# A step's maxima ahead of the last step's scaling in VectorE's order (context attention of a two-layer decoder)

## The chip, the cores and the metric

The kernel runs on one core of one Trainium2 chip. A core has five engines that run beside each other, each in its own order: TensorE (PE, with its weight loads PEld), VectorE (DVE), ScalarE (ACT), GpSimd (POOL) and SyncE (SP), which issues transfers. They wait for each other by semaphores. The metric is the device time of one execution in microseconds (us); the median of three runs is compared.

## What is computed

The reference is a decoder of two layers, each made of self-attention, attention with a context and a feed-forward part, every one followed by a layer norm. The input x is 8 sequences of 512 tokens and 256 features in float32, the context 8 sequences of 64 tokens. The second layer's feed-forward part is a mixture of 8 experts of which each token takes 2. The part that matters here is the second layer's context attention: the keys and values of a sequence are joined with those of its context, so a token attends to 512 + 64 positions, with 8 heads of 64.

```python
def _L1_xattn_ref(x1, x2, Wq1, Wk1, Wv1, Wk2, Wv2, Wo, bo):
    ...
    q1 = split_heads(x1 @ Wq1, N1)
    k1 = split_heads(x1 @ Wk1, N1)
    v1 = split_heads(x1 @ Wv1, N1)
    k2 = split_heads(x2 @ Wk2, N2)
    v2 = split_heads(x2 @ Wv2, N2)
    k = jnp.concatenate([k1, k2], axis=1)
    v = jnp.concatenate([v1, v2], axis=1)
    sim = jnp.einsum('bihd,bjhd->bhij', q1.astype(jnp.float32), k.astype(jnp.float32)) * scale
    attn = jax.nn.softmax(sim, axis=-1)
    out = jnp.einsum('bhij,bjhd->bihd', attn, v)
    out = out.reshape(B, N1, h * d)
    return out @ Wo + bo
```

Around it stands `x = _layernorm(x + _L1_xattn_ref(...))`, and then the experts' part, which begins with a norm of its own and a router: two experts of each token by the greatest of 8 probabilities.

## The kernel before, in words

The stage is the phase "l1_context". It works in 128 steps n = 16b + 4c + i: sequence b (0 to 7), pair of heads c (0 to 3), tile i of 128 tokens (0 to 3). In this text (b,c,i) is such a step. The phase is scheduled by hand: on TensorE, VectorE, ScalarE and GpSimd the instructions run in the order in which the program writes them. A step is written so:

- l1x_scaling of step n-1: VectorE takes the reciprocals of the two heads' sums (L1261) and multiplies their probabilities by them, 128 x 576 each, in place (L1263, in the helper `scaled`).
- l1x_scores of step n: TensorE computes the scores of two heads (L1560), each 128 x 576 in two halves, into two PSUM tiles "s"; VectorE takes the negated maximum of each head (nm, L1564).
- l1x_transposes of step n-2, with the exponentials of step n in between: TensorE transposes the 128 context columns (L1586), and ScalarE copies them out (L1587). Then ScalarE makes the exponentials of both heads out of PSUM, with their sums (l1x_exps, L1570). Then TensorE transposes the 512 other columns of each head (L1592); VectorE copies out the first head's, ScalarE the second's (L1593).
- for i below 3, l1x_project: one of queries, keys and values of the next pair of heads (L1525, L1539; copied by ScalarE; for the keys VectorE adds the context's, L1534). For i = 3, l1x_values: the product with the values (L1602, L1607) of the pair of heads before this one, ready two steps earlier.
- side work of single steps. In (b,2,2) l1_turn transposes the next sequence's x, in two groups of four (L1065, copied by ScalarE). The list `aside` brings, for the sequence that has just ended, l1x_out and the router: in the next sequence at (0,3) a sum on GpSimd; at (1,0) and (1,1) the output product o_out (L1646) with the sum and the statistics on VectorE (L1648, L1619, L1620, L1623); from (1,2) to (2,1) two norms on VectorE (L1632 and its like); at (2,2) route_transposes (tZ, L1709, two groups, copied by ScalarE); at (2,3) route_odds (o_r, L1724); at (3,0) to (3,2) shares, picks and seconds on VectorE; at (3,3) route_places: TensorE's o_rank (L1779, L1782), VectorE's ranks down to row numbers (L1784 to L1792) and, on GpSimd's queue, eight scatters of token rows to rows_in (L1794). The sequence before the last follows a denser list, in which tZ comes at step 120, o_r at 121, o_rank at 124, and the first table of the experts' tiles in the steps behind it.

What sets the order around the change are PSUM's banks. The ring "s" has two tiles, and a step's scores take both, so the scores of step n+1 wait until both exponentials of step n have read theirs. The ring "t" has three tiles, and a step's transposes take all three: the context columns first, then the two heads; side work takes the next ones in turn. So whatever takes a fourth and fifth tile in a step needs those of the context columns and of the first head, which VectorE's copy frees. The tile of probabilities p has four buffers, the columns nm, sums and rsum four each.

After the phase the experts' phase loads rows of rows_in (L1926) and weights for 71 tiles, each with an up product (L1958) and a down product (L1975). Its first loads wait for the scatters.

Of the kernel before, what the change touches and what calls it, by code (L numbers as in the profile page):

```python
# [50 lines left out]
def decoder_kernel(ctx: ExitStack, tc: tile.TileContext, a: dict, out: bass.AP):  # L51
# [31 lines left out]
    def phase(name):  # L83

        return tc.tile_pool(name=name, bufs=2, side="right", reuse_waits="tile")
# [4 lines left out]
    def s_tile(name):  # L90
        return pp["s"].tile([P, 2, 512], F32, tag="s", name=name)
# [206 lines left out]
    def p_tile(n=S, bufs=3):  # L298
        return ph.tile([P, 2, n], F32, tag="p", name="p", bufs=bufs)
# [4 lines left out]
    def col(name, n):  # L304
        return work.tile([P, n], F32, tag=name, name=name, bufs=4)
# [801 lines left out]
    with phase("l0_context_ffn") as ph, tc.manual_schedule(engines=ALL):  # L1107
# [8 lines left out]
        steps_ = [(b, i) for b in range(NB) for i in range(NT)]  # L1116
# [33 lines left out]
        for n in range(2 * NT, len(steps_) + 3):  # L1150
            b, i = n // NT, n % NT
# [353 lines left out]
    def l1x_context_values(b):  # L1505

        o = t_tile("o_v2").rearrange("p i n -> p (i n)")
        for kc in range(KC):
            pe.matmul(o, lhsT=ctxT[:, kc, b * S2 : (b + 2) * S2], rhs=wv2[:, kc, :], start=(kc == 0), stop=(kc == KC - 1))
        both = work.tile([P, S], F32, tag="lat", name="both")  # L1510
        act.copy(both, o)
        for n in range(2):
            vx = vxs[(b + n) % 4]
            for j in range(2):
                heads = [t.rearrange("p (h two n) -> p h two n", two=2, n=S2)[:, :, j, :] for t in (vx, both)]
                sp.dma_start(out=heads[0][S2 * j : S2 * (j + 1)], in_=heads[1][S2 * n : S2 * (n + 1)])

    def l1x_project(b, c, what):

        xT = live["xT", b]  # L1520
        cols = slice(c * P, (c + 1) * P)
        o = o_tile("o_qkv")
        if what < 2:
            for kc in range(KC):
                pe.matmul(o, lhsT=(wq1, wk1)[what][:, kc, cols], rhs=xT[:, kc, :], start=(kc == 0), stop=(kc == KC - 1))  # L1525
        if what == 0:
            q = ph.tile([P, S], F32, tag="q", name="q")
            act.mul(q, o, 0.125)
            live["q", b, c] = q
        elif what == 1:  # L1530
            k = ph.tile([P, S + 2 * S2], F32, tag="k", name="k")
            act.copy(k[:, S2 : S2 + S], o)
            for h, at in ((0, S2 + S), (64, 0)):
                dve.tensor_copy(k[h : h + 64, at : at + S2], k2[h : h + 64, c, b * S2 : (b + 1) * S2])  # L1534
            live["k", b, c] = k
        else:
            for j in range(NT):
                for kc in range(KC):
                    pe.matmul(  # L1539
                        o[:, j * P : (j + 1) * P],  # L1540
                        lhsT=xT[:, kc, j * P : (j + 1) * P],
                        rhs=wv1[:, kc, cols],
                        start=(kc == 0),
                        stop=(kc == KC - 1),
                    )
            v = ph.tile([P, NT, P], F32, tag="vc", name="vc", bufs=3)
            act.copy(v.rearrange("p j n -> p (j n)"), o)
            live["v", b, c] = v

    def l1x_scores(b, c, i):  # L1550
        q, k = live["q", b, c], live["k", b, c]
        p = p_tile(S + S2, bufs=4)
        sums = col("sums", 4)
        nm = col("nm", 2)
        ss = [s_tile("s_sc")[:, :, 0:HALF] for _ in range(2)]
        for t in range(2):
            for j, s in enumerate(ss):
                h = 64 * j
                at = S2 * (1 - j) + HALF * t
                pe.matmul(  # L1560
                    s[:, t, :], lhsT=q[h : h + 64, i * P : (i + 1) * P], rhs=k[h : h + 64, at : at + HALF], start=True, stop=True
                )
        for j, s in enumerate(ss):
            dve.tensor_reduce(nm[:, j : j + 1], s, AX.XY, ALU.max, negate=True)  # L1564
        live["s", b, c, i] = ss, p, sums, nm
# [9 lines left out]
    def l1x_scaling(b, c, i):  # L1575
        p, sums = live["p", b, c, i]
        scaled(p, sums, S + S2)

    def l1x_transposes(b, c, i, meanwhile):
        p, _ = live.pop(("p", b, c, i))  # L1580
        p = p.rearrange("p j n -> p (j n)")
        if i == 0:
            live["pt", b, c] = pts[c % 2], ph.tile([P, S], F32, tag="pt2", name="pt2")
        pt, pt2 = live["pt", b, c]
        t = t_tile("tP2")[:, 0, :]
        pe.transpose(t, p[:, S : S + P], ident)  # L1586
        act.copy(pt2[:, i * P : (i + 1) * P], t)  # L1587
        meanwhile()
        for j, copy in ((0, dve.tensor_copy), (1, act.copy)):
            t = t_tile("tP")  # L1590
            for k in range(NT):
                pe.transpose(t[:, k, :], p[:, (S + P) * j + k * P : (S + P) * j + (k + 1) * P], ident)  # L1592
            copy(pt[j][:, :, i * P : (i + 1) * P], t)  # L1593
# [413 lines left out]
    with phase("l1_context") as ph, tc.manual_schedule(engines=ALL):  # L2007
        vxs = [ph.tile([P, S], F32, name=f"vx{n}", bufs=1) for n in range(4)]
        for vx in vxs:
            pool.memset(vx, 0.0)  # L2010
        steps_ = [(b, c, i) for b in range(NB) for c in range(4) for i in range(NT)]
        aside = {}
        l1x_context_values(0)
        for what in range(3):
            l1x_project(0, 0, what)
        for n in range(len(steps_) + NT):
            b, c, i = n // (4 * NT), n // NT % 4, n % NT
            if 1 <= n <= len(steps_):
                l1x_scaling(*steps_[n - 1])
            if n < len(steps_):  # L2020
                l1x_scores(b, c, i)
            meanwhile = partial(l1x_exps, b, c, i) if n < len(steps_) else nothing
            if 2 <= n < len(steps_) + 2:
                l1x_transposes(*steps_[n - 2], meanwhile)
            else:
                meanwhile()
            if i < 3:
                nb, nc_ = (b, c + 1) if c < 3 else (b + 1, 0)
                if nb < NB:
                    l1x_project(nb, nc_, i)  # L2030
            elif n >= NT:
                pb, pc = steps_[n - NT][:2]
                l1x_values(pb, pc)
                if pc == 3 and pb < NB - 1:
                    after = [
                        *l1x_out(pb),
                        *(partial(f, pb) for f in (route_transposes, route_odds, route_shares, route_picks, route_seconds, route_places)),
                    ]
                    ats = list(range(len(after)))
                    if pb == NB - 2:  # L2040
                        ats = [0, 1, 2, 3, 3, 4, 4, 5, 6, 7, 7, 8, 9, 10, 11, 12, 13, 13]
                        early_pieces = early_blocks()
                        after.extend([lambda: next(early_pieces, None)] * 4)
                        after.extend(partial(moe_load, m, tables_rows) for m in range(AHEAD))
                    for at, piece in zip(ats, after):
                        aside.setdefault(n + at, []).append(piece)
            if (c, i) == (2, 2) and b + 1 < NB:
                for kc in range(KC):
                    l1_turn(b + 1, kc)
            if (b, c, i) == (NB - 1, 2, 1):  # L2050
                last = l1x_out(b)
                last.pop(0)()
            if (c, i) == (1, 1) and b % 2 and b + 1 < NB:
                l1x_context_values(b + 1)
            for piece in aside.pop(n, []):
                piece()
        for n in sorted(aside):
            for piece in aside[n]:
                piece()
        for piece in last[:4]:  # L2060
            piece()
        last_route.extend(
            [
                lambda: (last[4](), last[5]()),
                nothing,
                nothing,
                partial(route_transposes, NB - 1),
                lambda: (route_odds(NB - 1), route_shares(NB - 1)),
                lambda: (route_picks(NB - 1), route_seconds(NB - 1)),
                partial(route_places, NB - 1),  # L2070
            ]
        )
# [139 lines left out]
```

## Time and profile before

| what | us |
|---|---|
| median of three runs | 3152.14 (3150.56 to 3152.29) |
| the profiled execution | 3156.77 |
| its span, first to last instruction | 3155.1 |
| TensorE busy | 3063.9 (97%) |
| VectorE busy | 1920.7 (61%) |
| ScalarE busy | 1642.3 (52%) |
| GpSimd busy | 1101.3 (35%) |

The groups of the page that belong to the steps of this stage, with the line, the engine, what is written from what, the count, then busy us and mean ns of one, then idle us of the engine ahead of them and what ended it:

```profile
L1263 DVE TENSOR_SCALAR p<-p,rsum 128x576 f32<-128x576 f32 (+4 forms) x768 | 297.1, 429 | 13.6
L1570 ACT ACTIVATE p<-s_sc,nm 128x576 f32<-128x576 f32 x256 | 187.4, 737 | 101.8 <-DVE nm L1564 101.1
L1564 DVE TENSOR_REDUCE nm<-s_sc 128x1 f32<-128x576 f32 x256 | 181.4, 750 | 73.2 <-PE s_sc L1560 73.2
L1560 PE MATMUL s_sc<-k,q 64*128 64x288 f32 x1024 | 174.2, 433 | 9.7 <-ACT p L1570 9.7
```

L1263 is a helper's line that the self-attention uses too: 256 of the 768 are this stage's. An idle time is charged to the engine that waited, not to the end of the program; whether it counts is seen in the chain of waits, which follows the last instruction back to what released each one.

### The profile page before, as it was taken

The numbers are of one execution on the slowest core, as the hardware profiler recorded it, in microseconds if no ns is written. First come the engines' busy times: TensorE is split into PE (matmuls) and PEld (weight loads), VectorE is DVE, ScalarE is ACT, GpSimd is POOL, SyncE is SP. The second block draws the span as 40 slices with busy tenths as digits, with TensorE's granted clock in tenths as the row PEclk, the third lists the DMA queues.
The fourth block names the chain that finished last, engine by engine and source line by source line (L and its number), as shares of the span: only waits on it lengthen the run. The fifth ranks groups of instructions, "written<-read, shape, count | busy, mean of one in ns | idle before, by whom it ended". The sixth has DMA issues, their size and how long they took to land.

```text
span 3155.1 us, 54217 instructions
## 1 busy us (share of the span) xinstructions
PE 3063.9 (97%) x19598; PEld 2029.3 (64%) x19598; DVE 1920.7 (61%) x6331; ACT 1642.3 (52%) x3507; POOL 1101.3 (35%) x992
## 2 busy tenths in 40 slices
PE   8999999999999999999999999999999999999995
PEld 3444444455666677677767765666666558888885
DVE  6888888876553767767677746766766773110112
ACT  4555555557664666766676656555545543222222
POOL 5988888934432222222222210011111112221222
PEclk8999999999999999999999999999999999999998
DMA  5000111101006963333332310000000016766674
GB/s 165 28 28 28 41 45 44 35 6 43 6 3 170 255 132 48 41 41 41 42 45 38 42 43 1 16 16 25 22 18 21 21 51 210 226 193 180 185 238 148
DMA packets 170975, 235.25 MB, mean 75 GB/s; under 512 B 31915, under 2 KB 134059, under 8 KB 170709
## 3 DMA queue, kind: packets, MB, share of 16 engines
q1 hardware_dynamic: 144692, 179.91, 18.2%
q0 software_dynamic: 25584, 51.57, 11.5%
q8 instruction: 155, 2.54, 0.3%
q14 instruction: 112, 0.91, 0.1%
q10 hardware_dynamic: 432, 0.33, 0.0%
HBM read 136.03 MB, written 61.12 MB: 62 GB/s over the span
## 4 chain that ended last, share of the span: by engine, by line
PE 83%; DVE 6%; ACT 4%; DMA 2%; SPq 2%; issue 1%; POOL 0%; POOLq 0%; DVEq 0%; ACTq 0%
PE o_y L1975 7%; PE s_h L1958 7%; PE s_sc L480 5%; PE s_sc L1560 4%; PE o_pv L1345 4%; PE s_sc L1283 4%; PE tP L1332 4%; PE o_pv L576 4%; PE o_out L1369 4%; PE o_out L1039 3%; PE o_pv L1602 3%; PE s_q L1080 3%; PE o_qkv L1525 3%; PE tP L1592 3%; PE s_h L1015 2%; PE s_st L556 2%
## 5 line engine op out<-in xcount | busy, mean ns | idle before, releaser
L565 ACT ACTIVATE pt<-s_st 128x1024 f32<-128x1024 f32 x256 | 248.3, 1022 | 263.5 <-PE s_st L561 263.5
L1101 POOL DMA_DIRECT2D qk<-turned x256 | 202.8, 1168 | 520.2 <-PE tP L1332 319.4
L489 DVE CUSTOM_DVE_ANT_0 scored<-s_sc,decay 128x512 f32<-128x512 f32 x492 | 314.5, 686 | 54.3 <-PE s_sc L480 52.5
L1310 ACT ACTIVATE p<-p,nm 128x128 f32<-128x128 f32 (+3 forms) x512 | 282.6, 554 | 61.4 <-DVE nm L1296 61.4
L1263 DVE TENSOR_SCALAR p<-p,rsum 128x576 f32<-128x576 f32 (+4 forms) x768 | 297.1, 429 | 13.6
L1296 DVE CUSTOM_DVE_ANT_0 p<-s_sc,tabs 128x128 f32<-128x128 f32 (+3 forms) x512 | 215.6, 487 | 124.9 <-PE s_sc L1283 124.9
L1995 DVE TENSOR_SCALAR y<-o_y,share 128x256 f32<-128x256 f32 x71 | 34.2, 483 | 403.3 <-PE o_y L1975 403.3
L1958 PE MATMUL s_h<-xnT,we 128*128 128x256 f32 (+1 forms) x1248 | 258.8, 361 | 0.0
L1975 PE MATMUL o_y<-we,h 128*128 128x256 f32 x1136 | 251.4, 379 | 0.0
L1996 POOL DMA_INDIRECT total<-y,to x71 | 109.8, 1546 | 386.2 <-DVE y L1995 193.4
L1570 ACT ACTIVATE p<-s_sc,nm 128x576 f32<-128x576 f32 x256 | 187.4, 737 | 101.8 <-DVE nm L1564 101.1
L1975 PEld LDWEIGHTS o_y<-we,h 128*128 128x128 f32 x1136 | 215.3, 190 | 29.0
L1958 PEld LDWEIGHTS s_h<-xnT,we 128*128 128x128 f32 x1248 | 215.4, 190 | 23.9 <-ACT xnT L1937 0.2
L1564 DVE TENSOR_REDUCE nm<-s_sc 128x1 f32<-128x576 f32 x256 | 181.4, 750 | 73.2 <-PE s_sc L1560 73.2
L1332 PEld LDWEIGHTS tP<-ident,p 128*128 128x128 f32 x1280 | 144.8, 141 | 82.6 <-PE s_sc L1283 41.7
L480 PE MATMUL s_sc<-k,q 32*128 32x512 f32 x1024 | 188.9, 648 | 6.0 <-DVE mx L489 4.9
L1794 POOL DMA_INDIRECT rows_in<-z,irow x64 | 63.2, 988 | 374.2 <-DVE hit L1789 267.1
L1560 PE MATMUL s_sc<-k,q 64*128 64x288 f32 x1024 | 174.2, 433 | 9.7 <-ACT p L1570 9.7
L1332 PE MATMUL tP<-ident,p 128*128 128x128 f32 x1280 | 175.2, 276 | 0.1
L1937 ACT ACTIVATE xnT<-tZ,gb 128x256 f32<-128x256 f32 (+1 forms) x78 | 42.6, 546 | 237.5 <-PE tZ L1936 237.5
L1283 PE MATMUL s_sc<-qk 64*128 64x128 f32 (+3 forms) x1024 | 157.5, 443 | 3.8 <-DMA qk<-turned 3.3
L1965 ACT ACTIVATE h<-s_h 128x1024 f32<-128x1024 f32 x71 | 72.7, 1024 | 155.7 <-PE s_h L1958 155.7
(341 smaller groups left out, 6456.0 us busy)
## 6 DMA issues: line engine op xcount, KB each, us to landing
we<-in_mo_w SPq DMA_DIRECT2D x78, 1024.0 KB
rows_in<-zero SPq DMA_DIRECT2D x64, 530.0 KB
qk<-turned POOLq DMA_DIRECT2D x256, 128.0 KB, 4.3
coef<-in_ff_upw SPq DMA_DIRECT2D x40, 256.0 KB
coef<-in_ff_dnw SPq DMA_DIRECT2D x40, 256.0 KB
xr<-rows_in SPq DMA_DIRECT2D x32, 265.0 KB
x<-in_x SPq DMA_DIRECT2D x8, 512.0 KB
total<-x SPq DMA_DIRECT2D x8, 512.0 KB
```

Of the source, the lines that this page charges most:

```text
L480: pe.matmul(pairs[h // 2][:, h % 2, :], lhsT=q[r, i * P : (i + 1) * P], rhs=k[r, :], start=True, stop=True)
L489: dve.tensor_tensor_reduce(out=rows_[h], in0=pairs[h // 2][:, h % 2, :], in1=decay[:, i, :], scale=1.0, scalar=-3.0e38, op0=ALU.mult, op1= ...
L565: act.activation(pt, s, AF.Exp, scale=1.0 / 16.0)
L1101: pool.dma_start(out=qk[h : h + 32], in_=other[g : g + 32], accum_op=ALU.add)
L1263: dve.tensor_scalar(p[:, j, 0:n], p[:, j, 0:n], rsum[:, j : j + 1], None, ALU.mult)
L1283: pe.matmul(ss[j][:, at : at + n], lhsT=qk[h : h + 64, 0, i * P : (i + 1) * P], rhs=qk[h : h + 64, 1, 0:n], start=True, stop=True,)
L1296: dve.tensor_tensor_reduce(out=p[:, j, :], in0=ss[j], in1=causal[:, S - (i + 1) * P : S], scale=-1.0 / 8.0, scalar=3.0e38, op0=ALU.add, op ...
L1310: act.activation(p[:, j, :], p[:, j, :], AF.Exp, bias=nm[:, j : j + 1], scale=-1.0, accum_out=sums[:, j : j + 1])
L1332: pe.transpose(t[:, n, :], p[:, j, at * P : (at + 1) * P], ident)
L1560: pe.matmul(s[:, t, :], lhsT=q[h : h + 64, i * P : (i + 1) * P], rhs=k[h : h + 64, at : at + HALF], start=True, stop=True)
L1958: pe.matmul(s[:, j, :], lhsT=w1[:, c, f * P : (f + 1) * P], rhs=xnT[:, c, :], start=(c == 0), stop=(c == KC - 1),)
L1975: pe.matmul(o, lhsT=h[:, f, i * P : (i + 1) * P], rhs=w2[:, f, :], start=(f == 0), stop=(f == 7),)
```

## The change

In the loop over the steps two blocks change places: the scores and maxima of step n are now written ahead of the scaling of step n-1. Nothing else changes, and no instruction is added or removed. TensorE's order stays as it was, since the scaling has no instruction there; ScalarE and GpSimd have none in either block. On VectorE the two maxima of step n stand ahead of the reciprocal and the two multiplications of step n-1.

```diff
         for n in range(len(steps_) + NT):
             b, c, i = n // (4 * NT), n // NT % 4, n % NT
+            if n < len(steps_):
+                l1x_scores(b, c, i)
             if 1 <= n <= len(steps_):
                 l1x_scaling(*steps_[n - 1])
-            if n < len(steps_):
-                l1x_scores(b, c, i)
             meanwhile = partial(l1x_exps, b, c, i) if n < len(steps_) else nothing
```

## The prediction

> **What bounds the kernel now.** I read the page's chain first: TensorE holds 83% of it, VectorE 6%, ScalarE 4%. Then the stage that the change touches, the second layer's context attention (its maxima, L1564, start at 1877.5 us and end near 2583), in windows of 100 us. Columns: stretch, length, then busy us and instructions of each engine, granted clock, DMA.
>
> ```profile
> PE 83%; DVE 6%; ACT 4%; DMA 2%; SPq 2%; issue 1%; POOL 0%; POOLq 0%; DVEq 0%; ACTq 0%
> ...
> 2100.00:2200.00 100.00, 98.28 (x572) 60.71 (x571) 66.59 (x167) 54.17 (x131) 12.53 (x12) 1.00 0.06 20
> ```
>
> TensorE is busy 98.3 of 100 us at the full granted clock, VectorE 67. So a change of VectorE's order is worth only what TensorE waits for it, and I looked for those waits: in the chain of waits of the stage, then in the timeline of each place. An ordinary step (no side work) takes 4.02 us of TensorE time, and in it VectorE waits 0.66 us for the scores and 0.42 us for the exponentials (the timeline at 2050 us): nothing is lost there. The chain leaves TensorE at two places of every sequence from the second on. Here they are for sequence 2 (start us, us, what):
>
> ```profile
> 2039.92 0.34 PE o_rank L1782 x3
> 2040.27 0.02 issue
> 2040.29 0.20 DVE rank L1784
> ...
> 2041.70 0.17 DVE irow L1792
> 2041.87 0.08 DVE rsum L1261
> 2041.95 0.02 issue
> 2041.97 1.06 DVE p L1263 x2
> 2043.03 0.67 DVE nm L1564
> ...
> 2043.79 0.84 ACT p L1570 x2
> 2044.63 0.04 issue
> 2044.67 1.96 PE s_sc L1560 x8
> ...
> 2075.31 0.70 DVE r L1648
> ...
> 2077.51 0.98 DVE p L1263 x2
> 2078.49 0.68 DVE nm L1564
> ...
> 2079.25 0.84 ACT p L1570 x2
> 2080.09 0.04 issue
> 2080.13 1.96 PE s_sc L1560 x8
> ```
>
> Place A, step (b,0,0): side work of the step before (route_places) starts on VectorE when TensorE ends o_rank, which is just ahead of this step's scores. So the side work (2040.29 to 2041.87), then the scaling of the last step's probabilities, then the maxima stand between those scores and the exponentials, and the next scores, which need the score banks back, come late. Place B, step (b,1,2): the same with l1x_out's sum and statistics behind o_out. The stall is read from the scores: TensorE idle before them, plus their 1.96 us against 1.24 undisturbed in the timeline. A: idle 0.40 once (step 33) and 0.31 five times, plus 0.72, which is 1.12 and five times 1.03. B: idle 0.75 to 0.78, plus 0.72, so 1.5, at steps 23, 39, 55, 71, 87, 103 and 119.
>
> **The change part by part.** It adds and removes no instruction and no DMA. In each of 128 steps VectorE's order goes from scaling(n-1), maxima(n), copy(n-2), side work(n) to maxima(n), scaling(n-1), copy(n-2), side work(n); "copy" is the one of the first transposed half (L1593). One scaling is a reciprocal and two multiplications. At B, step 38, its reciprocal starts at 2077.32 and the maxima behind it at 2078.41, so it delays them by 1.08 to 1.09. By the same rows it is 1.17 at step 32 and 1.08 at the other A's.
>
> *The maxima come earlier only where VectorE waited in between.* From one maxima to the next VectorE does the same work in both orders: maxima, scaling, copy, side work. So where VectorE runs from step to step without a wait, the next maxima come at the same time as before. The gain needs side work that starts late for another reason; then the scaling that was ahead of the maxima has long been done in the new order. At A VectorE sits idle 4.00 us for o_rank, at B 2.25 us or more for o_out, and both can take 1.08 us of scaling in.
>
> - A: the maxima come 1.17 and 1.08 earlier, the stall is 1.12 and 1.03, so it goes whole: 1.12 + 5 x 1.03 = 6.3 us.
> - B: 1.08 of 1.5 goes, at the six steps 23 to 103: 6.5 us. The rest stays, because the next late maxima (step 39) follow step 38's by pure VectorE work.
> - B at step 119 gives nothing. From o_out's end at 2532.8 to the copy of step 120 VectorE never waits, so that copy ends at the same time in either order, and a transposition of the router (L1709) needs its bank:
>
> ```profile
> 2549.22 0.68 DVE L1593 COPY pt<-tP 128x512 f32<-128x512 f32 x1
> ...
> 2549.96 0.65 PE L1709 MATMUL tZ<-ident,z 128*128 128x128 f32 x4 [0.33 <-DVE pt L1593]
> ...
> 2570.10 0.68 DVE L1593 COPY pt<-tP 128x512 f32<-128x512 f32 x1
> ...
> 2570.92 0.19 DVE L1784 TENSOR_TENSOR rank<-o_rank,count 128x32 f32<-128x32 f32 x1
> ```
>
> The 1.08 us won at step 119 are waited there.
>
> **What is pushed back.** Copy(n-2) and the side work now stand behind the scaling. In an ordinary step they begin 1.1 us later, since that scaling used to run while TensorE did the scores. Who waits for them:
>
> - The copy frees one of three transposition banks. It would end 2053.8 instead of 2052.70 (step 34); TensorE comes back to the bank at 2054.73. Cover: 0.9 us.
> - Step (b,2,2): the second turn of x needs that bank already in the same step. It starts at 2100.07 (step 42); the copy would end at 2100.8. That is 0.76 late, but 0.32 to 0.33 us of waiting follow anyway (the second tZ group at 2101.56), and by the rows of 0.43 us a group the run would then reach tZ's second group at 2101.70 and the scores at 2102.14, against 2102.15 now. Cost 0; without that cover 0.76 x 6 = 4.6. I take 0 and keep +4.6 as the bound.
> - The scaling itself is needed a step later by the transposes: it ends 2.6 us behind the scores, and they start at 4.0.
> - The end of the stage. At step 124 (last rows of the second fence) copy, then rank: only 0.14 us lie between, and the scaling ahead of them ran in a wait of 1.17 us. The copy would end at 2571.9, so route_places starts 0.95 us later. Eight scatters of rows_in (L1794) follow it one by one, first at 2572.27, last landing at 2599.82; the experts' loads wait for them, and the chain runs through them. So 0.95 us are lost. For the same reason the stalls of steps 126 and 127 (1.62 and 0.22 us idle) are not shortened: here the work of VectorE is what counts.
> - Startup, steps 1, 2 and 4: the scores are stretched by the exponentials, and maxima start 1.77 us after their start (step 4) where the matmul that they need ends at 1.71. Gain 0.
>
> Sum: 6.3 + 6.5 - 0.95 = 11.8 us. Made against the profiled execution: 3156.77 us, of which 3155.1 are the span; it lies 4.6 us (0.15%) above the median of the runs, 3152.14. So 3145.0 for that one, and 3140.3 for the median.
>
> [...] Gaps between the eight scatters of the last fence's step are 2.78 to 3.81 us; the longest, up to 2579.10, spans the scaling at 2577.03 to 2577.97. [...]
>
> **The rivals.**
> 1. *One half only.* If A or B is held by something that hides behind the stall (TensorE's next step finds another wait), 6.4 us less: 11.8 - 6.4 = 5.4, so 3146.7. For it: B's next maxima are late anyway. Against: at both places the chain names the maxima.
> 2. *Handed back.* VectorE's work is the limit over the whole stretch, as in the last sequence: nothing gained, 0.95 lost, 3153.1. For it: the steps behind A and B are full of side work. Against: the idle 4.00 and 2.25 us.
> 3. *The scatters move.* The five scalings of the tail come at other times against the scatters. Each can lengthen or spare a gap by up to its 0.95 us: between one spared (3139.4) and three hit (3143.2). [...]
> 4. *Slower: the bank.* If the copy comes later than the cover of 0.9 us beyond its present end, TensorE waits at the first transposes of each ordinary step. There are 72: 96 steps without the value products, less 14 with o_out, 7 with turns and 3 with the last routing. That is 7.2 us for each 0.1 us. The gain is gone when the copy ends 0.93 + 0.16 us behind its forecast end (0.16 is 11.8 / 72); at 0.3 over the cover it is 22 - 12 = +10 us, 3162. For it: a step fills all three banks. Against: the move is one scaling of 1.1 us, and no multiplication of L1263 took over 0.68 us, where the median is 0.45.
>
> **How the numbers follow.** The forecast 0.66, half only 0.09, handed back 0.05, scatters 0.12, bank 0.08. The likeliest's own range is 3137 to 3144 (the runs spread 1.7 us; shifts of 1.08 read to 0.05 at twelve places). The range goes down to 3137 and up to 3148, which takes in the half and most of the bound of +4.6 at the turns. About 0.2% (6.3 us) is what a measurement of this kernel can tell from no change. Faster: forecast and scatters, 0.78; same: half and handed back, 0.14; slower: the bank, 0.08.
>
> **What would show it.** Scores at steps 33, 49 and on 1.24 us long, with no idle before them; at steps 23, 39 and on idle gone, about 0.4 us of stretch left; the chain no longer through L1263 there; in step 124 rank 0.95 us behind o_rank's end (now it follows at once), and the first scatter with it; the second turn at (b,2,2) late by 0.76 and the next scores not. Wrong would be any wait of the tP transposes (L1592) for the copy in ordinary steps, or maxima at A that don't move.

## The result, and the profile after

The changed kernel takes 3143.4 us (median of seven runs, 3134.84 to 3145.41), the kernel before 3152.29 us (seven runs, 3150.07 to 3155.93): 8.9 us less, a ratio of 0.9966 with a 95% interval of 0.9956 to 0.9977. Run once more beside other kernels it took 3139.26 us against 3152.69, a ratio of 0.9961 (0.9948 to 0.9975). The profiled execution fell from 3156.77 to 3144.25 us, its span from 3155.1 to 3142.5.

These are the lines of the page's chain (shares of the span by engine), and of a 100 us window in the middle of the stage, which answer to the first lines shown for the kernel before:

```profile
PE 85%; DVE 5%; ACT 4%; DMA 3%; issue 1%; POOL 0%; SPq 0%; POOLq 0%; DVEq 0%; ACTq 0%
...
2091.00:2191.00 100.00, 99.65 (x585) 62.38 (x584) 67.61 (x171) 52.38 (x128) 12.58 (x12) 0.99 0.06 20
```

TensorE is now busy 99.65 of 100 us where it was 98.28. VectorE does as much as before, 67.6 us against 66.6. Next, the chain of waits of the changed kernel at places A and B of sequence 2 (start us, us, what):

```profile
2029.05 0.87 PE o_rank L1782 x8
2029.92 1.17 PE s_sc L1560 x8
...
2033.94 1.19 PE s_sc L1560 x8
...
2063.77 1.17 PE s_sc L1560 x8
2064.94 0.26 PE tP L1586
2065.20 0.87 PE tP L1592 x8
2066.08 1.79 PE o_qkv L1539 x16
2067.86 1.64 PE s_sc L1560 x8
```

The chain no longer leaves TensorE at either place: no rsum, no p, no nm stands in it. The scores behind A (step 33, 2033.94) take 1.19 in the chain where they took 1.96. Those behind B (step 39, 2067.86) take 1.64, so part of their stretch is left. The timeline of step 32 shows the cause (start us, us, engine, line):

```profile
2031.37 0.17 DVE L1792 CAST irow<-place 128x4 int32<-128x4 f32 x1
...
2031.45 1.41 DVE L1564 TENSOR_REDUCE nm<-s_sc 128x1 f32<-128x576 f32 x2
...
2032.78 0.15 DVE L1261 RECIPROCAL rsum<-sums 128x2 f32<-128x2 f32 x1
...
2033.87 1.26 PE L1560 MATMUL s_sc<-k,q 64*128 64x288 f32 x8
```

The maxima start 0.08 us behind the start of the last side work, and the reciprocal of the last step's scaling comes behind them. Before, the reciprocal and the multiplications stood in that gap.

### The stage step by step

Executions differ before the stage begins (its first scores start at 1876.24 us before and at 1867.24 after, in code that is the same), so everything is counted from the start of the stage's first scores, "S0". Step 118 is the last before the losses, step 124 routes the last but one sequence; "121" is the time from the scores of step 120 to those of 121; "rank" is the time from o_rank's end in step 124 to L1784; then the first of the eight scatters behind it, the landing of the last, and the end of the program.

| kernel | 118 | 121 | 124 | rank | first scatter | last lands | end |
|---|---|---|---|---|---|---|---|
| before | 656.47 | 5.45 | 691.25 | 0.04 | 696.03 | 723.58 | 1278.8 |
| changed | 646.56 | 7.82 | 682.23 | 0.87 | 687.84 | 717.64 | 1275.3 |
| changed, again | 643.20 | 7.82 | 678.87 | 0.87 | 684.48 | 708.25 | 1266.5 |
| A alone | 650.53 | 5.44 | 685.31 | 0.04 | 690.10 | 715.21 | 1275.7 |
| B alone | 649.95 | 5.44 | 684.73 | 0.04 | 689.51 | 717.50 | 1277.6 |
| A and B | 644.61 | 5.45 | 679.39 | 0.04 | 684.18 | 710.22 | 1268.8 |
| tail alone | 656.40 | 7.81 | 692.05 | 0.87 | 697.66 | 723.88 | 1281.7 |
| sum early | 643.19 | 5.93 | 676.97 | 0.87 | 682.58 | 708.62 | 1264.9 |
| copy first | 643.17 | 6.37 | 677.78 | 0.87 | 683.39 | 711.15 | 1267.8 |
| old tail | 643.21 | 5.45 | 677.99 | 0.04 | 682.77 | 706.76 | 1265.0 |
| joined | 645.67 | 5.08 | 679.00 | 0.04 | 683.79 | 710.63 | 1266.1 |

Up to the first scatter the numbers repeat to some hundredths between kernels that share an order, apart from what is told below: stretches in which TensorE's granted clock was 0.50 ("half clock", in "changed" and "joined"), and a collision in "joined". Behind it they scatter by several us: the eight scatters took 23.8 to 29.8 us from first issue to last landing, and the two extremes are two profiles of the same changed kernel.

### The profile page after: what moved, and what is told of

Its sections match the earlier page's. It is cut to its first block, busy times and chain, and to the rows that moved or that the text cites. A ratio compares the mean times of both kernels' runs of the same rounds, so it can differ in the third digit from the quotient of the medians.

```text
span 3142.5 us, 54242 instructions
## 1 busy us (share of the span) xinstructions
PE 3056.2 (97%) x19598; PEld 2029.7 (65%) x19598; DVE 1918.8 (61%) x6331; ACT 1643.6 (52%) x3507; POOL 1101.5 (35%) x992
## 4 chain that ended last, share of the span: by engine, by line
PE 85%; DVE 5%; ACT 4%; DMA 3%; issue 1%; POOL 0%; SPq 0%; POOLq 0%; DVEq 0%; ACTq 0%
PE o_y L1975 7%; PE s_h L1958 7%; PE s_sc L480 5%; PE s_sc L1283 5%; PE s_sc L1560 5%; PE o_pv L1345 5%; PE tP L1332 4%; PE o_pv L576 4%; PE o_out L1369 4%; PE o_out L1039 4%; PE o_pv L1602 3%; PE s_q L1080 3%; PE o_qkv L1525 3%; PE tP L1592 3%; PE s_h L1015 2%; PE s_st L556 2%
```

## The experiments

The edits of "copy first" and of "joined" are shown against the kernel before, all others against the changed kernel; "..." stands for lines left out.

### A alone

```diff
+            ahead = 32 <= n < 128 and n % 16 == 0
-            if 1 <= n <= len(steps_):
+            if 1 <= n <= len(steps_) and not ahead:
                 l1x_scaling(*steps_[n - 1])
             if n < len(steps_):
                 l1x_scores(b, c, i)
+            if ahead:
+                l1x_scaling(*steps_[n - 1])
```

> New order at the six A steps alone (32, 48, 64, 80, 96, 112), old order elsewhere. Theory (the gain is the scaling taken out from between late side work and the maxima): the maxima of these steps come about 1.08 us earlier, the scores of steps 33, 49 and on lose 1.1 us of stall each, B's scores keep 1.5 us; 6.5 to 7 us less inside the stage, and the stage's end as before the change (rank in step 124 at once behind o_rank, the multiplications at step 119 0.95 us in all). Rival 1 (the new order gains a little in every step): far less than half, some 6/128 of the stage's gain. Rival 2 (the gain of the medians is half-clock stretches of TensorE that fell elsewhere): the stage no shorter, once steps at half clock are left out.

Measured: 3147.0 us against 3154.57, ratio 0.9973 (0.9961 to 0.9985). At each A the scores gained 1.16 us (step 33) or 1.07 to 1.08. Two steps on, 0.01 to 0.20 us were lost again: in step 33 and its like, in the old order, the scaling stood ahead of maxima that were now due at once, so that the scores of step 50, say, took 1.43 us where they take 1.24 in the changed kernel. Step 118 came 5.9 us earlier; B kept its idle 0.77 and its scores of 1.96 us, and the tail stayed as it was. Six steps of 128 give nearly half of the stage's gain, so the gain is not spread over the steps, and it is there in a stage that ran at full clock up to step 125 (5.94 us at step 118, 5.93 at the first scatter, where a stretch of half clock cost 1.68).

### B alone

The same edit with another set of steps:

```diff
+            ahead = 22 <= n < 112 and n % 16 == 6
```

> New order at six B steps alone (22, 38, 54, 70, 86, 102). Theory: the scores of steps 23, 39 and on lose 1.09 us of 1.5 each, 6.5 us inside the stage; A's scores keep 1.03 to 1.12; the tail as before the change. Rival 1: some 6/128 of the gain. Rival 2: no gain in the stage outside steps at half clock.

Measured: 3146.14 us against 3154.57, ratio 0.9976 (0.9964 to 0.9988). Step 118 came 6.52 us earlier, 1.06 to 1.09 at each of the six. The timeline of TensorE at step 33 and at step 39:

```profile
2033.36 1.96 PE L1560 MATMUL s_sc<-k,q 64*128 64x288 f32 x8 [0.40 <-ACT p L1570]
...
2067.98 1.71 PE L1560 MATMUL s_sc<-k,q 64*128 64x288 f32 x8
```

A's stall is the one of the kernel before, to the hundredth; at B the idle time of 0.77 us is gone and 0.47 us of stretch (1.71 against 1.24) remain.

### A and B

```diff
+            ahead = n in (22, *range(32, 118, 16), *range(38, 112, 16))
```

> New order at the six A and the six B steps, old order in the other 116, the first sequence and everything from step 113 on included. Theory (losses sit in steps 119 to 124, gains at A and B): 13.1 to 13.5 us less by step 118; at step 120 and 124 nothing pushed back, so rank follows o_rank at once, and the scores of step 121 are not late; against the changed kernel some 3 us less up to the first scatter. Time about 13 us under the kernel before, 3139. Rival (the stage's end is set by the scatters whatever the order): the first scatter comes earlier, but the last lands as late as in the changed kernel, time 3143.

Measured: 3142.12 us against 3154.57, ratio 0.9955 (0.9941 to 0.9968). Step 118 came 11.86 us earlier, not 13.1 to 13.5: the steps behind A, in the old order, gave back 0.02 to 0.26 us each, and step 38 another 0.12. Rank followed at once, step 121 was not late, and the first scatter came 11.85 us earlier than in the kernel before. Some 3 us less than the changed kernel were expected up to there; that holds against its first profile, with its half clock (684.18 against 687.84), while against the second (684.48) it is 0.30. The rival, which had the last scatter land as late as in the changed kernel, isn't decided: it landed at 710.2, against 717.6 in the changed kernel's first profile and 708.3 in its second, so these landings can't be compared from single profiles.

### Tail alone

```diff
+            ahead = 118 <= n < 128
```

> New order at steps 118 to 127 alone. Theory: 1.09 gained at step 119, lost again and 1.3 more at step 121 because the multiplications of step 118 meet GpSimd's sum (L1636) and take 2.8 us in place of 0.95, and rank in step 124 comes 0.95 us later behind o_rank; so the first scatter 1.5 to 2.5 us later than in the kernel before, time 2 to 5 us over it. Rival (the long multiplications were chance): only 0.95 later.

Measured: up to step 118 the stage is the one before (656.40). Then 1.09 us are gained at step 119 and 2.36 lost at 121, 0.40 come back at 122, rank is 0.83 us later, and the first scatter is 1.63 us later than before, as expected. The multiplications of step 118 took 2.83 us again, so the rival, chance, falls. The time missed its expectation: 3153.45 us against 3154.57, ratio 0.9995 (0.9985 to 1.0004), and not 2 to 5 us slower. A loss of 1.6 us at the first scatter can't be found in the time, with scatters behind it that vary by six.

### Sum early

```diff
-            if (b, c, i) == (NB - 1, 2, 1):
+            if (b, c, i) == (NB - 1, 1, 0):
                 last = l1x_out(b)
                 last.pop(0)()
```

> The changed kernel, with GpSimd's sum for the last sequence (L1636) issued five steps earlier, so that it is done long before step 119. Theory (in step 119 the multiplications stand still until the sum is done): they take 0.95 us in place of 2.83, and the scores of step 121 are 1 to 1.5 us later against step 120 than before the change, in place of 2.4; what is left is the 1.09 won at step 119, given back. Stage and first scatter 1 to 1.5 us earlier than in the changed kernel. Rival (the multiplications are slow for what they read): still 2.8 us.

The timeline of the changed kernel at this place, and then that of this one (start us, us, engine, line):

```profile
2523.73 2.37 POOL L1636 TENSOR_TENSOR xb<-x,bo 128x1024 f32<-128x1024 f32 x1
...
2524.04 2.83 DVE L1263 TENSOR_SCALAR p<-p,rsum 128x576 f32<-128x576 f32 x2
...
2526.93 0.33 PE L1586 MATMUL tP<-ident,p 128*128 128x128 f32 x1 [0.58 <-DVE p L1263]
...
2532.34 0.66 PE L1709 MATMUL tZ<-ident,z 128*128 128x128 f32 x4 [2.00 <-ACT pt L1593]
```

```profile
2518.99 1.01 POOL L1624 TENSOR_TENSOR rs<-ve,mhalf 128x4 f32<-128x4 f32 x1 [5.57 <-DVE ve L1623]
...
2519.95 0.10 POOL L1765 MEMSET both<- 128x8 f32 x1
...
2520.28 0.95 DVE L1263 TENSOR_SCALAR p<-p,rsum 128x576 f32<-128x576 f32 x2
...
2526.69 0.66 PE L1709 MATMUL tZ<-ident,z 128*128 128x128 f32 x4 [0.82 <-ACT pt L1593]
```

With the sum (L1636) running, two multiplications take 2.83 us; without it 0.95. TensorE waited 0.58 us for the probabilities in the first case, and 2.00 us at the router's second group, where it is 0.82 in the second. Step 121 follows step 120 after 5.93 us instead of 7.82, and the first scatter comes 1.90 us earlier than in the changed kernel's second profile. Both are more than expected: step 121 is 0.48 us later against step 120 than in the kernel before, not 1 to 1.5, so the 1.09 us won at step 119 are not all given back. The median is 3135.18 us against 3152.69, ratio 0.995 (0.9935 to 0.9965). The rival falls: the multiplications read the same data in both.

### Copy first

```diff
             if n < len(steps_):
                 l1x_scores(b, c, i)
-            if 1 <= n <= len(steps_):
-                l1x_scaling(*steps_[n - 1])
...
             else:
                 meanwhile()
+            if 1 <= n <= len(steps_):
+                l1x_scaling(*steps_[n - 1])
             if i < 3:
```

> Maxima, then the copy of the first transposed half, then the scaling, then side work. Theory: A and B as in the changed kernel (1.1 and 1.09 us each), because the maxima stand where they stood; the copy ends 1.1 us earlier in every step; step 121 about 1.1 us less late than in the changed kernel, since the copy is what the second tZ group waits for; rank in step 124 still 0.95 us behind o_rank, since scaling and copy both stand ahead of it. Rival (the late copy costs TensorE time in ordinary steps too): 0.1 us or more in each ordinary step, 7 us or more over the stage.

Measured: 3139.72 us against 3152.69, ratio 0.9963 (0.9951 to 0.9975). Step 118 stands at 643.17, where the changed kernel's second profile has 643.20: in ordinary steps the later copy costs TensorE nothing, and the rival falls. Step 121 is 1.45 us less late than in the changed kernel (6.37 against 7.82; 1.1 was expected). The reason given for the 1.1 was not quite right: in the changed kernel the router's second group waits for ScalarE's copy (the line with 2.00 above), and only here for VectorE's again; and the multiplications of step 118 began later beside the sum and took 2.25 us in place of 2.84. Rank is 0.87 us behind o_rank (0.95 was expected).

### Old tail

```diff
+            ahead = 1 <= n < 118
```

> New order in steps 1 to 117, old order from 118 on. Theory: 0.23 us at the start, 6.6 at A, 6.5 at B, 13.3 in all by step 118 (more than with A and B alone, where the step behind an A fell back into the old order and lost 0.1 to 0.26 us); then the tail of the kernel before: rank at once behind o_rank, step 121 not late. Some 13 us under the kernel before, and 2 to 3 under the changed kernel. Rival (steps at half clock come with the new order): again stretches of half clock near steps 60 and 92, 1.7 us each.

Measured: 3136.75 us against 3152.69, ratio 0.9953 (0.994 to 0.9967). Step 118 came 13.26 us earlier, and the whole gain is still there at the first scatter (13.26), because the tail is that of the kernel before. The medians lie 15.9 us under the kernel before and 2.5 under the changed one. No stretch of half clock lay in the middle of the stage, so the rival finds no support here.

### The changed kernel again

Nothing is edited.

> The changed kernel once more, nothing edited. [...] The third gap of the last eight scatters but one, 4.73 us in the changed kernel's first profile, stays above 4 if the order makes it, and falls to some 3 if it was chance.

Measured: step 118 came 13.27 us earlier. The stretches of half clock at steps 60 and 92 (3.4 us and 1.68 us lost each in the first profile) are gone; all other steps of the stage start as in the first profile, to 0.04 us (7.82 and 0.87 in the table), and the two multiplications of step 118 took 2.84. The third gap between the scatters was 2.89 us instead of 4.73, so that was chance. The end is 8.8 us earlier than in the first profile, counted from S0, with the same program.

Here is step 124's rank with the copy ahead of it, in this kernel and in the one with the old tail:

```profile
2549.52 0.68 DVE L1593 COPY pt<-tP 128x512 f32<-128x512 f32 x1
2550.12 0.18 DVE L1784 TENSOR_TENSOR rank<-o_rank,count 128x32 f32<-128x32 f32 x1
2551.46 1.04 POOL L1794 DMA_INDIRECT rows_in<-z,irow  x1 [1.82 <-DVE hit L1789]
```

```profile
2554.29 0.68 DVE L1593 COPY pt<-tP 128x512 f32<-128x512 f32 x1
...
2555.10 0.19 DVE L1784 TENSOR_TENSOR rank<-o_rank,count 128x32 f32<-128x32 f32 x1
...
2556.46 1.04 POOL L1794 DMA_INDIRECT rows_in<-z,irow  x1 [1.17 <-DVE hit L1789]
```

In the first the rank starts when the copy is done, in the second 0.13 us after the copy's end, when o_rank is done.

### Joined

```diff
+            late = 1 <= n < 124
-            if 1 <= n <= len(steps_):
+            if 1 <= n <= len(steps_) and not late:
                 l1x_scaling(*steps_[n - 1])
...
                 meanwhile()
+            if late:
+                l1x_scaling(*steps_[n - 1])
...
-            if (b, c, i) == (NB - 1, 2, 1):
+            if (b, c, i) == (NB - 1, 1, 0):
```

> What helped, joined: steps 1 to 123 in the order maxima, copy, scaling, side work; the old order from step 124 on; GpSimd's sum of the last sequence five steps earlier. Theory: 13.3 us by step 118, then step 121 follows step 120 after 5.4 to 5.9 us (7.8 in the changed kernel, 5.45 before), rank at once behind o_rank, and the first scatter 14.2 to 14.8 us earlier, counted from the stage's first scores, than in the kernel before (11.6 in the changed kernel's second profile, 13.3 to 13.5 in the two best so far). Time some 14.5 us under the kernel before. Rival (the tail of the old order is held by the scatters alone): first scatter as promised, and no less time than with the old tail.

Measured: 3138.93 us against 3151.49, ratio 0.9957 (0.9944 to 0.9971). Step 121 follows after 5.08 us and rank at once, but the first scatter came only 12.24 us earlier. Two things were lost on the way: 1.68 us in a stretch of half clock at step 108, and 0.79 us at step 117, where the early sum, back to back with the one before it, met a scaling (without these two it would have been 14.7, as expected):

```profile
2504.43 5.92 DVE L1263 TENSOR_SCALAR p<-p,rsum 128x576 f32<-128x576 f32 x2
2505.37 4.66 POOL L1636 TENSOR_TENSOR xb<-x,bo 128x1024 f32<-128x1024 f32 x2
```

The remedy had the same fault as the change: it moved a collision. The time is 12.6 us under the kernel before (14.5 was expected), no better than "sum early" or "old tail"; since the first scatter did not come as promised, the rival isn't decided. These two are the best versions: both beat the kernel before, and up to the first scatter they are 1.7 to 1.9 us ahead of the changed kernel (table). Their ratios' intervals overlap with the changed kernel's, so the time alone doesn't separate them.

## Why the prediction was right

The forecast was 11.8 us. Counted from S0, the first scatter came 11.55 us earlier in the changed kernel's second profile and 8.19 in the first, which lost 3.36 us at half clock; the medians fell by 8.9 and 13.4 us.

- **Where the gain sits** held: A and B and nowhere else, since each alone gave its part, and both together nearly all.
- **A's size**: forecast 6.3 us, found 1.16 + 5 x 1.07 = 6.5. The idle time before the scores was counted from zero, but undisturbed scores overlap the end of the matmul before them by 0.07 us.
- **B's size**: forecast 6.5 us, found 6.5; the rest of the stretch stays, as forecast (0.47 us of 1.5).
- **Step 119 gives nothing** was wrong, and in two ways. The 1.09 us are won and lost, but 1.3 more are lost at step 121, and 0.40 come back at 122: a net loss of 0.88 where 0 was forecast. The step that failed is "VectorE does the same work in both orders". It does the same instructions, but two of them took 2.83 us where they had taken 0.98, because they now ran beside GpSimd's sum. In the kernel before, the sum started just when they had ended:

```profile
2541.65 0.98 DVE L1263 TENSOR_SCALAR p<-p,rsum 128x576 f32<-128x576 f32 x2
2542.67 2.37 POOL L1636 TENSOR_TENSOR xb<-x,bo 128x1024 f32<-128x1024 f32 x1
2544.48 1.71 DVE L1632 TENSOR_SCALAR z<-x,mv,rs 128x256 f32<-128x256 f32 x4
```

  A move changes what an instruction runs beside, and I had looked at that for the scatters alone. The second way is the wait that was to eat the 1.09 us. With the sum out of the way ("sum early") the copy of step 120 does end about when it did (16.79 us behind step 118's scores, 17.20 in the kernel before), but the router's second group no longer waits for it; it waits for ScalarE's copy (the line with 0.82 above), since the banks are handed out in another order, see below. From step 118 to 124 that kernel takes 33.78 us and the kernel before 34.78, so 1.00 of the 1.09 is kept. Up to 0.34 of that is not the order's: the kernel before itself lost as much to the sum, whose end the four instructions of L1632 met (1.71 us, 1.37 in the changed kernel). No run has the old order with the early sum, so how much the order alone would keep there is open.
- **The end of the stage**: forecast 0.95 us later, found 0.83 (0.87 behind o_rank's end where it was 0.04).
- **Startup**: forecast 0, found 0.23, at step 1. I had taken the matmul that ends at 1.71 for the one that the maxima need. In the changed kernel the maxima of step 1 start 1.45 us after the scores, and the sixth of the eight matmuls ends at 1.40: in this step, this is the one.
- **The second turn at (b,2,2)**: cost 0 was right, the way to it not quite. The bank that it waits for is no longer the first head's. The ring of three hands out banks in another order in the changed kernel, an effect that the diff doesn't show. In the program's instruction lists the waits of the two transposes of an ordinary step have changed places:

```
-L1592 Matmult tP<-ident,p 128x128 [waits DVE_49]
-L1592 Matmult tP<-ident,p 128x128 x3
-L1592 Matmult tP<-ident,p 128x128 [waits Activation_49]
+L1592 Matmult tP<-ident,p 128x128 [waits Activation_49]
+L1592 Matmult tP<-ident,p 128x128 x3
+L1592 Matmult tP<-ident,p 128x128 [waits DVE_49]
```

  So the turn waits for ScalarE's copy: 0.35 us, not 0.76, and the later waits go, as forecast; step 43 starts where it did against step 42. Nor does the diff show that the program gets 25 more instructions, waits of TensorE's (54242 on its page, 54217 before); the work of each engine stays as it was.
- **The rivals.** "Half only" and "handed back" fall with A alone and B alone. "The bank" falls: no ordinary step is longer, to 0.01 us. "The scatters move" is left open as a cause: their gaps vary by chance more than by the order (23.8 and 29.8 us in two profiles of one kernel). That a scaling lengthens a gap by its 0.95 us was my estimate from one gap of 3.81 us, and no run shows it apart from chance. Work of GpSimd beside a multiplication counted at another place: the two of step 118 took 2.83 us beside the sum, where they had taken 0.98.

The forecast for the time, 3140.3 us, lies 3.1 us under the first median and 1.0 over the second. That the sum came out within 0.3 us up to the first scatter (11.55 against 11.8) is partly luck: the 0.88 missed at step 119 were in part made up by 0.2 more at A, 0.23 at startup and 0.12 less at the end. And what a single profile adds, stretches of half clock and the scatters, is larger than the terms that I missed.

## What to carry to other kernels

Moving an instruction ahead in an engine's order paid here only where the engine stood idle for another reason between the two places (VectorE 4.00 us at A, 2.25 us or more at B); from one wait-free step to the next the sum of work is the same in any order, as long as each instruction takes as long as it did, so look for the idle time first. Then list what each moved instruction will run beside, the work of GpSimd above all (two multiplications of 0.95 us took 2.83 beside its sum), and what had used the slack that it now takes. To judge a gain of a third of a per cent, count from the first instruction of the stage and compare steps: the times of whole runs can't tell such terms apart.

## What the runs showed that I had not expected

*Half clock.* Here are windows of 1 us in the first profile of the changed kernel, just behind o_r of step 59 (stretch, length, busy of PE, PEld, DVE, ACT, POOL, granted clock, DMA):

```profile
2189.00:2190.00 1.00, 1.00 (x10) 0.57 (x7) 0.26 (x2) 0.23 (x1) 0.00 (x0) 0.93 0.00 0
2190.00:2191.00 1.00, 1.00 (x6) 1.00 (x5) 1.00 (x2) 0.57 (x2) 0.00 (x0) 0.50 0.00 0
2191.00:2192.00 1.00, 1.00 (x6) 0.99 (x5) 0.96 (x4) 1.00 (x3) 0.00 (x0) 0.50 0.00 0
2192.00:2193.00 1.00, 1.00 (x2) 0.34 (x1) 1.00 (x3) 0.73 (x3) 0.00 (x0) 0.50 0.00 0
2193.00:2194.00 1.00, 1.00 (x3) 0.19 (x1) 0.39 (x3) 0.00 (x0) 0.00 (x0) 0.86 0.00 0
```

Read with such windows over the whole span, the granted clock falls to 0.50 in stretches of 3.4 or 6.8 us: 34.0 us in all in the profile before, 30.6 and 17.0 in the two of the changed kernel, the end of the program left out. Some lie near the same place in all three (one at 681 to 685 us, one at 2555 to 2576), others don't. Each 3.4 us cost 1.68 here. Ahead of the stage it was 27.2 us before and 10.2 after, which, at half its length, is an estimated 8.5 of the 9.0 us by which the stage began earlier in the changed kernel's first profile than in the kernel before; in other pairs it explains less. In the middle of the stage such stretches came three times, at steps 60, 92 and 108, each time behind o_r, whose matmuls are 8 columns wide; twice in "changed", once in "joined", in none of the other nine profiles, "changed, again" among them. TensorE was busy by the records in the windows above (1.00 in each), and no run shows what makes the clock fall. Whether the new order, with fewer stalls, makes them likelier is open: too few were seen.

*A sum that stops a multiplication.* The first of the two multiplications at step 118 started 0.31 us after GpSimd's sum and lasted until 0.35 us behind its end: the two took 2.83 us in place of 0.95. In "joined", where the 5.92 us stand behind two sums, the multiplication that was held had started 0.50 us ahead of the first sum, and a scatter was then in progress on GpSimd (from 2504.39 us, for 0.96). Some multiplications were longer beside a scatter too: over the eleven profiles, 32 multiplications of the stage that met no sum took 0.60 to 0.76 us, where 0.52 is the median, and each ended 0.26 us behind the end of a scatter's instruction. So in "joined" it may be the scatter that held it until the sum had begun.

Such a meeting cost nothing where there was slack: in "changed, again" two more multiplications were held by a sum behind a scatter, for 3.22 and 3.05 us (at 2409.37 and 2498.47 us), and no step started later for it than in the first profile, which had neither.
